# Later copies, joined stores and a longer-spread finish in the scan stage of an attention and selective-scan kernel

## The chip, the cores and the metric

The kernel runs on one core of one Trainium2 chip. The metric is the device time of one execution in microseconds (us). Before the change it is 35322.73 us, the median of three runs (35309.54 to 35332.95).

## The reference

The input x is a 256 x 256 grid of tokens with 128 channels. Layer 0 is a group norm, then row-wise attention with a bias, a mask and a gate, added to x. Layer 1, where the change is, does this on the result (shapes of this case, K = 4 directions, 256 inner channels, 16 states):

```python
xz = x @ w_in.T;  xi, z = split(xz);  z = silu(z)
xc = silu(depthwise_conv3x3(xi) + conv_b)
xs = [rows, columns, rows reversed, columns reversed] of xc      # L = 65536 tokens each
dts, Bs, Cs = split(xs @ x_proj)                                   # 8, 16, 16
delta = softplus(dts @ dt_w + dt_b)
for t in range(L):                                                 # for each direction, channel, state
    h = exp(delta[t] * A) * h + delta[t] * x[t] * B[t]
    y[t] = sum over states of h * C[t]      (+ D * x[t])
y = sum of the four directions, each put back in token order
out = x + (layernorm(y) * z) @ w_out.T
```

## The kernel before, in words

Lines are those of the kernel before. Layer 0 and the projection and convolution take the first fifth of the time and are not touched. What follows is one long software pipeline, written out by hand: within it the order of the instructions on every engine is the order in which the Python program issues them.

**Tiling.** The four directions are done one after the other, in the order 2, 1, 3, 0. A direction has 128 chunks of 512 tokens. A chunk has 8 steps (`g`, 0 to 7); a step does 32 channels x 16 states, laid out as 128 partitions (4 blocks of states x 32 channels) by 4 states (`NI`). So there are 4 scans of 128 x 512 in a step, and 4 *places* (`n`, 0 to 3) in the loop over them, 32 places in a chunk. Place 0 does the fourth state, which is kept apart (`dAl`, `bl`); places 1 to 3 do the others.

**One place** issues on ACT the exponential dA (L983; three PSUM buffers, two SBUF buffers for dAl), then pieces of the side work, then on DVE the scan (L1009). After place 1, DVE multiplies B with delta*x for the next step (`times_B`, L734, from `ur`, which PE spreads at L723). The fourth state gets its B*delta*x by another way: ACT scales a transposed delta*x (`bt`, L693), PE turns it back (`bl`, L705). At the end of a step GpSimd takes up the last state (`hst`, L1025) and multiplies with C in place (L1026, 7 buffers `bx`).

**Sums and copies.** After four steps, half a chunk, PE gathers over states and blocks into a PSUM tile `yp` (`sums`, L749, issued at step 5 for the first half and at step 1 of the next chunk for the second). ACT copies it to SBUF as `yo` (`evacuate`, L922), after which `begin_sums` may use the one `yp` buffer again. This copy is issued at place 0 of step 6 (first half) and of step 2 of the next chunk (second half).

**Side work** is written as generators. Each `yield` ends a piece. `prepare` (started at step 6, two chunks ahead) makes xs, B, C, delta and du = delta*x: copies of the turned x (L595), `pb` and `bc` (L599, L605), softplus by Abs, Relu, Exp and Ln, with Ln at L653, and four GpSimd operations, the last two being delta and delta*x (L659, L662). One piece of it goes to each place, so its Ln is at place 0 of step 2 of the next chunk and delta and delta*x are at place 3 of step 3. Ln and Exp each have a table load on ACT. `turn` (L675, L681) transposes du at step 4, place 3. Each generator in the list `later` gets one piece at every place, before `prepare` does.

**What goes into `later`.** In directions 2, 1 and 3 it is `store`, once per half: PE transposes yo, adding the sum of the directions before (`yl`, loaded by `load_sum`), ACT copies it into half of `yt`, and after the second half it goes to memory. In direction 0 it is `finish`, once per chunk: the sum of all directions (`ysum`, L771 and L776), a copy `ys` (L831), statistics on DVE (L838, L840), their root on GpSimd (`yrs`, `ynb`, L36, L37, L842, L843), normalisation on ACT (`yn`, L847), transposes (`tpz`, L861), weights and bias on ACT (`gz`, L868), the product with z on GpSimd (L872), the output projection with the residual (`po`, L878, L881), and a copy `xo` (L891) to the output.

**Queues.** All loads and stores of this stage go through the SP queue in issue order. PE, ACT, DVE and GpSimd each take their instructions in order too, so an instruction that waits holds what is issued after it on its engine.

Of the kernel before, what the change touches and what calls it, by code (L numbers as in the profile page):

```python
# [16 lines left out]
P = 128  # L17
# [6 lines left out]
DI = 256  # L24
# [42 lines left out]
def attention_and_scan_kernel(  # L67
# [498 lines left out]
        v = ap.rearrange("(i p w) d -> p w i d", p=P, w=S)  # L566
        return [v[:, w, :, :] for w in range(w0, w0 + T // S)]

    loaded, prepared, scanned, summed, turned, products_of = {}, {}, {}, {}, {}, {}

    def load(q):
        k, a = steps[q]
        xt = io.tile([P, 4, DI], F32, name="xtok")
        src = tokens(xc_d, k, a)
        n = 4 // len(src)
        for w, s in enumerate(src):
            nc.sync.dma_start(xt[:, n * w : n * w + n, :], s)
        loaded[q] = xt

    def prepare(q):  # L580

        k, a = steps[q]
        xt = loaded.pop(q)
        xs = io.tile([P, 2, T], F32, name="xs")
        tps = []
        for h in range(2):
            tp = sps.tile([P, T], F32, name="tps", tag="mm")
            for j in range(4):
                nc.tensor.transpose(
                    tp[:, j * P : (j + 1) * P], xt[:, j, h * P : (h + 1) * P], ident  # L590
                )
            tps.append(tp)
            yield
        for h, tp in enumerate(tps):
            nc.scalar.copy(xs[:, h, ::-1] if k >= 2 else xs[:, h, :], tp)  # L595
            yield
        pb = sps.tile([R + 2 * NS, T], F32, name="pb", tag="mm")
        for h in range(2):
            nc.tensor.matmul(  # L599
                pb, xw_in[:, k, h, :], xs[:, h, :], start=(h == 0), stop=(h == 1)  # L600
            )
        yield
        yield
        bc = io.tile([R + 2 * NS, T], F32, name="bc", bufs=1)
        nc.scalar.copy(bc, pb)  # L605
        bc_d = sd.tile([2 * NS, T], F32, name="bc_d")
        nc.sync.dma_start(bc_d, bc[R:, :])
        yield


        e = io.tile([P, 2, T], F32, name="e", bufs=1)
        delta = io.tile([P, 2, T], F32, name="delta", bufs=1)
        pvs = []
        for h in range(2):
            pv = sps.tile([P, T], F32, name="pv", tag="mm")
            nc.tensor.matmul(  # L616
                pv, dtw_s[:, k, h * P : (h + 1) * P], bc[:R, :], start=True, stop=True
            )
            pvs.append(pv)
        yield  # L620
        yield
        for h, pv in enumerate(pvs):
            nc.scalar.activation(e[:, h, :], pv, AF.Abs, bias=dtb_s[:, k, h : h + 1])
            nc.scalar.activation(delta[:, h, :], pv, AF.Relu, bias=dtb_s[:, k, h : h + 1])
            yield
        tp = sps.tile([P, 4, R + 2 * NS], F32, name="tpb", tag="mm")
        for b in range(4):
            nc.tensor.transpose(
                tp[:, b, :], bc[:, b * P : (b + 1) * P], ident[: R + 2 * NS, : R + 2 * NS]
            )  # L630
        nc.scalar.activation(e, e, AF.Exp, scale=-1.0)
        B_r = io.tile([P, NB, T], F32, name="B_r")
        C_r = io.tile([P, NI, T], F32, name="C_r")
        for m, t, ni in ((0, B_r, NB), (1, C_r, NI)):
            for j in range(4):
                n = m * NS + NI * j
                nc.sync.dma_start(
                    t[32 * j : 32 * j + 32],
                    bc_d[n : n + ni, :].unsqueeze(0).to_broadcast([32, ni, T]),
                )  # L640
        yield
        lg = io.tile([P, 2, T], F32, name="lg", bufs=1)
        nc.scalar.activation(lg, e, AF.Identity, bias=1.0)
        yield
        du = io.tile([P, 2, T], F32, name="du")
        nc.scalar.activation(du, lg, AF.Identity, bias=neg_one)
        B_t = io.tile([P, 4, R + 2 * NS], F32, name="B_t")
        nc.scalar.copy(B_t, tp)
        yield
        nc.gpsimd.tensor_tensor(e, e, du, ALU.subtract)  # L650
        yield
        yield
        nc.scalar.activation(lg, lg, AF.Ln)  # L653
        for _ in range(NI - 1):
            yield
        nc.gpsimd.tensor_tensor(lg, lg, e, ALU.add)  # L656
        for _ in range(NI):
            yield
        nc.gpsimd.tensor_tensor(delta, delta, lg, ALU.add)  # L659
        de_d = sd.tile([DI, T], F32, name="de_d")  # L660
        nc.sync.dma_start(de_d.rearrange("(h p) t -> p h t", p=P), delta)
        nc.gpsimd.tensor_tensor(du, delta, xs, ALU.mult)  # L662
        prepared[q] = xs, de_d, du, B_r, C_r, B_t
# [111 lines left out]
            else:  # L775
                nc.tensor.matmul(o, yo, ident, start=False, stop=True, skip_group_check=True)  # L776

    def store(q, yo, h):

        k, a = steps[q]  # L780
        yt, yl = scanned[q], summed.get(q)
        hs_ = slice(h * P, (h + 1) * P)
        yield
        tp = sps.tile([P, 4, P], F32, name="tpy", tag="mm")
        add_sum(
            tp,
            None if yl is None else yl[:, :, hs_],
            [(tp[:, j, :], yo[:, j * P : (j + 1) * P]) for j in range(4)],
        )
        yield  # L790
        yield
        nc.scalar.copy(yt[:, :, hs_], tp)
        if h == 1:
            dst = tokens(y_d[k], k, a)
            n = 4 // len(dst)
            for w, s in enumerate(dst):
                nc.sync.dma_start(s, yt[:, n * w : n * w + n, :])
            del scanned[q]
            summed.pop(q, None)

    def finish(q, yos):

# [1 line left out]

        a = steps[q][1]
        yl = summed.pop(q)

        def rest(n):
            for _ in range(n):
                yield  # L810

        yield
        zt = io.tile([P, 2, T], F32, name="zl", bufs=1)
        nc.sync.dma_start(zt, z_d[:, a : a + T].rearrange("(h p) t -> p h t", p=P))
        sums_ = []
        for g in range(2):
            ps = sps.tile([P, 2, DI], F32, name="ysum", tag="mm")
# [7 lines left out]
                ],  # L825
            )
            sums_.append(ps)
            yield from rest(2)
        ys = io.tile([P, 4, DI], F32, name="ys", tag="yt")
        for g, ps in enumerate(sums_):  # L830
            nc.scalar.copy(ys[:, 2 * g : 2 * g + 2, :], ps)  # L831
            yield
        st = io.tile([P, 4, 6], F32, name="yst")
        mv = io.tile([P, 4, 2], F32, name="ymv")
        rs = io.tile([P, 4], F32, name="yrs")
# [5 lines left out]
        rsqrt(nc, rs, mv[:, :, 1], 1e-5, neg_half)  # L841
        nc.gpsimd.tensor_tensor(nb, mv[:, :, 0], rs, ALU.mult)  # L842
        nc.gpsimd.tensor_scalar(nb, nb, -1.0, None, ALU.mult)  # L843
        yield from rest(3)
        yn = io.tile([P, 4, DI], F32, name="yn", tag="yl")
        for j in range(4):
            nc.scalar.activation(  # L847
                yn[:, j, :],
                ys[:, j, :],
                AF.Identity,  # L850
                bias=nb[:, j : j + 1],
                scale=rs[:, j : j + 1],
            )
            if j % 2:
                yield
        yield
        tps = []
        for h in range(2):
            tp = sps.tile([P, T], F32, name="tpz", tag="mm")
# [2 lines left out]
                    tp[:, j * P : (j + 1) * P], yn[:, j, h * P : (h + 1) * P], ident  # L862
                )
            tps.append(tp)
        yield from rest(2)
        gz = io.tile([P, 2, T], F32, name="gz", bufs=1)
        for h, tp in enumerate(tps):
            nc.scalar.activation(  # L868
                gz[:, h, :], tp, AF.Identity, bias=lnb_s[:, h : h + 1], scale=lnw_s[:, h : h + 1]
            )  # L870
            yield
        nc.gpsimd.tensor_tensor(gz, gz, zt, ALU.mult)  # L872
        yield from rest(11)
        xr = io.tile([P, 4, D], F32, name="xr", bufs=1)
        nc.sync.dma_start(xr, x2_d[a : a + T, :].rearrange("(j p) c -> p j c", p=P))
        yield from rest(12)
        po = sps.tile([P, 4, D], F32, name="po", tag="mm")
        nc.tensor.matmul(po, ident, xr, start=True, stop=True)  # L878
        for j in range(4):
            for h in range(2):  # L880
# [5 lines left out]
                    stop=True,  # L886
                    skip_group_check=True,
                )
        yield from rest(3)
        xo = io.tile([P, 4, D], F32, name="xo", bufs=1)  # L890
        nc.scalar.copy(xo, po)  # L891
        nc.sync.dma_start(out[a : a + T, :].rearrange("(j p) c -> p j c", p=P), xo)
# [27 lines left out]
    def evacuate(q, h):  # L920
        yo = wk.tile([P, T], F32, name="yo", bufs=2)
        nc.scalar.copy(yo[:, ::-1] if steps[q][0] >= 2 else yo, yps.pop((q, h)))  # L922
        yos[q, h] = yo
        if steps[q][0] == ORDER[-1]:
            if h == 1:
                later.append(finish(q, [yos.pop((q, 0)), yos.pop((q, 1))]))
                del prepared[q]
        else:
            if h == 0:
                scanned[q] = io.tile([P, 4, DI], F32, name="yt")  # L930
            later.append(store(q, yos.pop((q, h)), h))
            if h == 1:
                del prepared[q]

    def begin_sums(q, h):
        yps[q, h] = sps.tile([P, T], F32, name="yp", bufs=1)
# [6 lines left out]

    ctx.enter_context(tc.manual_schedule())
    load(0)
    load(1)
    preparing.append(prepare(0))
    drain(preparing)
    preparing.append(turn(0))
    drain(preparing)  # L950
    preparing.append(products(0, 0))
# [12 lines left out]
    for s, (q, g) in enumerate(all_steps):  # L964
        k, a = steps[q]
        nxt = all_steps[s + 1] if s + 1 < len(all_steps) else None
        if g == 1:
            drs[q, 1] = spread_delta(q, 1)
        if k != ORDER[0] and g == (4 if a else 5):
            summed[q] = load_sum(q)  # L970
        if g == 2 and q + 2 < NQ:
            load(q + 2)
# [5 lines left out]
        for n, i in enumerate((NB, *range(NB))):  # L978
# [4 lines left out]
            nc.scalar.activation(  # L983
                dA, dr, AF.Exp, scale=A_s[:, k, g // 4, g % 4, i : i + 1]
            )
            if n == 0 and g == 2 and q:
                evacuate(q - 1, 1)
                begin_sums(q, 0)
            if n == 0 and g == 6:
                evacuate(q, 0)  # L990
                begin_sums(q, 1)
            if n == 0 and g == 1 and q:
# [98 lines left out]
```

## Time and profile before

| stretch of the trace | us | PE | DVE | ACT | GpSimd (POOL) |
|---|---|---|---|---|---|
| whole span | 35280.6 | 74% | 84% | 71% | 73% |
| direction 2 | 6840 | 71% | 95% | 81% | 88% |
| directions 1 and 3 | 13610 | 71% | 96% | 81% | 88% |
| direction 0 | 7650 | 71% | 88% | 77% | 84% |

A chunk takes about 53.5 us in direction 2, 53.3 in directions 1 and 3, and 60.3 in direction 0. The costliest groups are GpSimd's product with C (4542 ns each, 18602.6 us in all), DVE's scans (1266 and 1259 ns, 20221.9 us together), and DVE's product with B (1729 ns, 7080.4 us).

In the lines of a profile, a group or timeline entry gives engine, line of the kernel, operation and tiles; `x4` is a count; a bracket such as `[2.50 <-ACT dA L983]` is the time the engine stood idle just before the instruction and what ended the wait. A line of the waits is "engine, tile, line <- who released it: us in total, times, longest".

### The profile page before, as it was taken

The numbers are of one execution on the slowest core, as the hardware profiler recorded it, in microseconds if no ns is written. First come the engines' busy times: TensorE is split into PE (matmuls) and PEld (weight loads), VectorE is DVE, ScalarE is ACT, GpSimd is POOL, SyncE is SP. The second block draws the span as 40 slices with busy tenths as digits, with TensorE's granted clock in tenths as the row PEclk, the third lists the DMA queues.
The fourth block names the chain that finished last, engine by engine and source line by source line (L and its number), as shares of the span: only waits on it lengthen the run. The fifth ranks groups of instructions, "written<-read, shape, count | busy, mean of one in ns | idle before, by whom it ended". The sixth has DMA issues, their size and how long they took to land.

```text
span 35280.6 us, 352910 instructions
## 1 busy us (share of the span) xinstructions
PE 26226.3 (74%) x109078; PEld 12390.7 (35%) x109078; DVE 29738.4 (84%) x29211; ACT 25019.2 (71%) x50182; POOL 25808.4 (73%) x11291
## 2 busy tenths in 40 slices
PE   5999899967677777777777777777777777777776
PEld 2555544433333333333333333333333333333333
DVE  7666611199999999999999999999999888888888
ACT  3555411188888788888888888888888777777777
POOL 4222200088888888888888888888888888888888
PEclk8999999977777777777777777777777777777777
DMA  3000111144444444444444444444444444444444
GB/s 128 29 29 29 32 62 62 65 104 104 106 104 105 103 105 107 115 114 116 114 115 115 117 115 115 116 114 116 115 116 115 112 109 112 110 109 111 110 111 102
DMA packets 2099611, 3516.78 MB, mean 100 GB/s; under 512 B 201384, under 2 KB 1187368, under 8 KB 2022832
## 3 DMA queue, kind: packets, MB, share of 16 engines
q1 hardware_dynamic: 2094832, 3492.87, 39.3%
q8 instruction: 857, 14.04, 0.2%
q14 instruction: 1042, 8.54, 0.1%
q10 hardware_dynamic: 2880, 1.34, 0.0%
HBM read 2754.17 MB, written 739.25 MB: 99 GB/s over the span
## 4 chain that ended last, share of the span: by engine, by line
POOL 49%; PE 23%; issue 11%; ACT 8%; DVE 8%; POOLq 0%; DMA 0%; ACTq 0%; DVEq 0%; SPq 0%
POOL bx L1026 34%; PE pc L471 6%; POOL du L662 3%; POOL delta L659 3%; PE yp L749 3%; DVE bx L1009 3%; POOL lg L656 2%; PE ur L723 2%; ACT dA L983 2%; DVE bx L734 2%; PE av L341 2%; POOL at L318 2%; POOL hst L1025 1%; ACT bt L693 1%; PE atp L330 1%
## 5 line engine op out<-in xcount | busy, mean ns | idle before, releaser
L1026 POOL TENSOR_TENSOR bx<-bx,C_r 128x2048 f32<-128x2048 f32 x4096 | 18602.6, 4542 | 334.0 <-POOL hst L1025 6.8
L1009 DVE TENSOR_TENSOR_SCAN bx<-dA,hst,bx 128x512 f32<-128x512 f32 x12192 | 15105.8, 1266 | 1234.0 <-ACT dA L983 1234.0
L723 PE MATMUL ur<-du,spread 128*128 128x512 f32 x8192 | 6490.3, 886 | 4357.5 <-DVE bx L734 4357.5
L983 ACT ACTIVATE dA<-dr,A_s 128x512 f32<-128x512 f32 x12288 | 8364.9, 686 | 1484.8 <-DVE bx L1009 1450.7
L734 DVE TENSOR_TENSOR bx<-B_r,ur 128x1536 f32<-128x1536 f32 x4096 | 7080.4, 1729 | 35.7 <-PE ur L723 35.7
L693 ACT ACTIVATE bt<-duT,B_t 128x128 f32<-128x128 f32 x16384 | 5664.6, 399 | 0.0
L1009 DVE TENSOR_TENSOR_SCAN bx<-dAl,hst,bl 128x512 f32<-128x512 f32 x4064 | 5116.1, 1259 | 576.5 <-ACT dAl L983 262.5
L749 PE MATMUL yp<-bx,gather 128*32 128x512 f32 x32768 | 4605.6, 690 | 12.3 <-POOL bx L1026 12.2
L705 PE MATMUL bl<-ident,bt 128*128 128x128 f32 x16384 | 3349.7, 340 | 1233.1 <-DVE bx L1009 1232.8
L705 PEld LDWEIGHTS bl<-ident,bt 128*128 128x128 f32 x16384 | 2317.8, 172 | 3379.3 <-DVE bx L1009 2623.5
L723 PEld LDWEIGHTS ur<-du,spread 128*128 128x128 f32 x8192 | 1695.1, 257 | 4988.9 <-DVE bx L734 4988.8
L1025 POOL COPY hst<-bx 128x4 f32<-128x4 f32 x4096 | 770.0, 188 | 3029.8 <-DVE bx L1009 2872.5
L983 ACT ACTIVATE dAl<-dr,A_s 128x512 f32<-128x512 f32 x4096 | 2936.7, 717 | 0.0
L318 POOL TENSOR_TENSOR at<-at,sm 128x2048 f32<-128x2048 f32 x256 | 922.3, 3603 | 2707.7 <-DVE sm L317 2568.4
L749 PEld LDWEIGHTS yp<-bx,gather 128*32 128x32 f32 x32768 | 1379.9, 126 | 3755.6 <-issue 3459.8
L675 PE MATMUL tpd<-ident,du 128*128 128x128 f32 x4096 | 979.3, 417 | 1842.7 <-POOL du L662 1842.7
L471 PE MATMUL pc<-xi,diag 128*128 128x512 f32 x4608 | 2031.5, 592 | 0.0
L488 DVE COPY xct<-pt 128x512 f32<-128x512 f32 x256 | 177.1, 692 | 1837.8 <-PE pt L487 1837.8
L616 PE MATMUL pv<-bc,dtw_s 8*128 8x512 f32 x2048 | 1201.8, 713 | 629.3 <-ACT bc L605 629.3
L681 ACT COPY duT<-tpd 128x512 f32<-128x512 f32 x1024 | 600.4, 586 | 1478.8 <-PE tpd L675 1478.8
L675 PEld LDWEIGHTS tpd<-ident,du 128*128 128x128 f32 x4096 | 775.0, 217 | 2474.0 <-POOL du L662 2474.0
L922 ACT COPY yo<-yp 128x512 f32<-128x512 f32 x1024 | 597.1, 583 | 1470.0 <-PE yp L749 1469.6
(166 smaller groups left out, 35061.1 us busy)
## 6 DMA issues: line engine op xcount, KB each, us to landing
dr<-de_d SPq DMA_DIRECT2D x4096, 256.0 KB
C_r<-bc_d SPq DMA_DIRECT2D x2048, 256.0 KB
B_r<-bc_d SPq DMA_DIRECT2D x2048, 192.0 KB
de_d<-delta SPq DMA_DIRECT2D x512, 512.0 KB
xtok<-xc_d SPq DMA_DIRECT2D x256, 512.0 KB
xtok<-xc_d SPq DMA_DIRECT2D x512, 256.0 KB
yl<-y_d SPq DMA_DIRECT2D x512, 256.0 KB
y_d<-yt SPq DMA_DIRECT2D x512, 256.0 KB
```

The costliest lines, as they stand in the source:

```text
L318: nc.gpsimd.tensor_tensor(at, at, sm.unsqueeze(3).to_broadcast([P, H, 2, S]), ALU.mult,)
L471: nc.tensor.matmul(pc, diag[:, h, t, :], xi[:, h, 2 * q + dy : 2 * q + dy + 2, dx : dx + S], start=(t == 0), stop=(t == 8),)
L616: nc.tensor.matmul(pv, dtw_s[:, k, h * P : (h + 1) * P], bc[:R, :], start=True, stop=True)
L675: nc.tensor.transpose(tp[:, b, h * P : (h + 1) * P], prepared[q][2][:, h, t0 : t0 + P], ident)
L693: nc.scalar.mul(bt[:, b, :, j, :], duT[:, b, h * P : (h + 1) * P].rearrange("t (g c) -> t g c", c=32), B_t[:, b, n : n + 1],)
L705: nc.tensor.transpose(bl[:, b * P : (b + 1) * P], bt[:, b, g % 4].rearrange("t j c -> t (j c)"), ident)
L723: nc.tensor.matmul(ur, spread[:, g % 4].rearrange("p j c -> p (j c)"), prepared[q][2][:, g // 4, :], start=True, stop=True,)
L734: nc.vector.tensor_tensor(bx[:, :NB, :], prepared[q][3], ur.unsqueeze(1).to_broadcast([P, NB, T]), ALU.mult,)
L749: nc.tensor.matmul(yp[32 * g : 32 * g + 32, :], gather, hc[:, i, :], start=(i == 0 and steps[q][0] != ORDER[0]), stop=True, skip_group_che ...
L983: nc.scalar.activation(dA, dr, AF.Exp, scale=A_s[:, k, g // 4, g % 4, i : i + 1])
L1009: nc.vector.tensor_tensor_scan(hs[:, i, :], dA, hs[:, i, :] if i < NB else bls.pop((q, g)), 0.0 if a == 0 else hst[:, g, i : i + 1], ALU.mult,
L1026: nc.gpsimd.tensor_tensor(hs, hs, prepared[q][4], ALU.mult)
```

## The change

It has four parts.

1. `evacuate` and `begin_sums` go one step later: from step 2 to step 3 (second half of the chunk before) and from step 6 to step 7 (first half). The `yo` copy is meant to meet sums that are done, and no longer to stand just ahead of the Ln at step 2. In consequence xs has three buffers, as `begin_sums` reads it later, and the token tile xtok one; the load of `yl` at a direction's first chunk goes from step 5 to step 7.
2. `store` is done once for both halves, after the second one: both sums at places 1 and 2, both copies two places later, then the store. `yt` is taken only there.
3. `finish` is spread: 58 places instead of 44, counted from place 0 of step 3. The statistics and their root come at step 4, place 2, after GpSimd's delta and delta*x instead of just ahead of them; the four `yn` at four places; `tpz` at step 1 of the chunk after, `gz` at step 2 behind Ln, the product with z at step 4, `po` at step 0 and `xo` at step 1 of the next chunk but one. The loads of z and of the residual are issued later as well.
4. The first load but one is issued after the first `prepare`.

```diff
-        xt = io.tile([P, 4, DI], F32, name="xtok")
+        xt = io.tile([P, 4, DI], F32, name="xtok", bufs=1)
-        xs = io.tile([P, 2, T], F32, name="xs")
+        xs = io.tile([P, 2, T], F32, name="xs", bufs=3)
...
-    def store(q, yo, h):
+    def store(q, yos):
...
+        yl = summed.pop(q, None)
+        yield
+        tps = []
+        for h, yo in enumerate(yos):
+            hs_ = slice(h * P, (h + 1) * P)
+            tp = sps.tile([P, 4, P], F32, name="tpy", tag="mm")
+            add_sum(
...
+            tps.append(tp)
+            yield
+        yield
+        yt = io.tile([P, 4, DI], F32, name="yt")
+        for h, tp in enumerate(tps):
+            nc.scalar.copy(yt[:, :, h * P : (h + 1) * P], tp)
+            yield
+        dst = tokens(y_d[k], k, a)
...
     def finish(q, yos):
...
-        yield
-        zt = io.tile([P, 2, T], F32, name="zl", bufs=1)
-        nc.sync.dma_start(zt, z_d[:, a : a + T].rearrange("(h p) t -> p h t", p=P))
+        yield
...
-            yield from rest(2)
+            yield
+        yield
         ys = io.tile([P, 4, DI], F32, name="ys", tag="yt")
         for g, ps in enumerate(sums_):
             nc.scalar.copy(ys[:, 2 * g : 2 * g + 2, :], ps)
             yield
+        zt = io.tile([P, 2, T], F32, name="zl", bufs=1)
+        nc.sync.dma_start(zt, z_d[:, a : a + T].rearrange("(h p) t -> p h t", p=P))
...
-        yield from rest(3)
+        yield from until(6, 11)
         yn = io.tile([P, 4, DI], F32, name="yn", tag="yl")
-        for j in range(4):
+        for j, now, then in ((0, 11, 12), (1, 12, 16), (2, 16, 17), (3, 17, 26)):
...
-            if j % 2:
-                yield
-        yield
+            yield from until(now, then)
...
-        yield from rest(2)
+        yield from until(26, 29)
         gz = io.tile([P, 2, T], F32, name="gz", bufs=1)
...
+        yield from until(31, 36)
         nc.gpsimd.tensor_tensor(gz, gz, zt, ALU.mult)
-        yield from rest(11)
+        yield from until(36, 40)
         xr = io.tile([P, 4, D], F32, name="xr", bufs=1)
...
-        yield from rest(12)
+        yield from until(40, 55)
...
-        yield from rest(3)
+        yield from until(55, 57)
...
-        if k != ORDER[0] and g == (4 if a else 5):
+        if k != ORDER[0] and g == (4 if a else 7):
...
-            if n == 0 and g == 2 and q:
+            if n == 0 and g == 3 and q:
                 evacuate(q - 1, 1)
                 begin_sums(q, 0)
-            if n == 0 and g == 6:
+            if n == 0 and g == 7:
                 evacuate(q, 0)
                 begin_sums(q, 1)
```

## The prediction

> **What bounds the kernel now.** I read the busy time by stage first, because three of the four directions end in a copy back to memory and the last in the finish. In the answer for the stretches of direction 2, directions 1 and 3, and direction 0 (columns: stretch, length, then PE, PEld, DVE, ACT, POOL busy, clock, DMA share, GB/s):
>
> ```profile
> 7060.00:13900.00 6840.00, 4827.52 (x19374) 2098.44 (x19374) 6520.32 (x5103) 5507.02 (x10706) 5988.14 (x2554) 0.73 0.43 104
> 13950.00:27560.00 13610.00, 9661.75 (x40914) 4352.18 (x40906) 13035.82 (x10223) 11036.19 (x21473) 11994.77 (x5112) 0.75 0.47 115
> 27610.00:35260.00 7650.00, 5407.26 (x23552) 2618.63 (x23551) 6713.80 (x6085) 5910.36 (x11496) 6452.51 (x3169) 0.78 0.45 110
> ```
>
> DVE is busy 95.3%, 95.8% and 87.8%: it bounds the first 384 chunks nearly, the last 128 not. So the question is what its idle time waits for. From the waits of DVE, the second stretch (first line), then the third:
>
> ```profile
> DVE bx L1009 <- ACT dA L983: 565.4, 255, 3.1
> ```
> ```profile
> DVE bx L1009 <- ACT dA L983: 391.4, 253, 3.0
> DVE bx L1009 <- ACT dAl L983: 262.5, 126, 2.9
> DVE bx L1009 <- ACT duT L681: 184.7, 82, 2.6
> DVE bx L1009 <- PE bl L705: 79.4, 97, 1.6
> ```
>
> Directions 1 and 3 have one wait per chunk, 565.4/255 = 2.22 us. (Direction 2, by the same view, 287.7 us on ACT in 127 chunks, some 0.2 us more on others: I use 2.5 in all.) Direction 0 has several, 918.0/127 = 7.23 us. The timeline of one chunk of direction 1 shows where; ACT and, below, DVE:
>
> ```profile
> 21002.47 0.72 ACT L983 ACTIVATE dAl<-dr,A_s 128x512 f32<-128x512 f32 x1
> 21004.73 0.58 ACT L922 COPY yo<-yp 128x512 f32<-128x512 f32 x1 [1.54 <-PE yp L749]
> 21005.33 1.28 ACT L653 ACT_TABLE_LOAD   x1
> 21006.63 1.06 ACT L653 ACTIVATE lg<-lg 128x1024 f32<-128x1024 f32 x1
> 21007.70 1.28 ACT L983 ACT_TABLE_LOAD   x1
> 21009.00 1.91 ACT L983 ACTIVATE dA<-dr,A_s 128x512 f32<-128x512 f32 x3
> ```
> ```profile
> 21009.72 1.28 DVE L1009 TENSOR_TENSOR_SCAN bx<-dA,hst,bx 128x512 f32<-128x512 f32 x1 [2.50 <-ACT dA L983]
> ```
>
> At step 2, place 0, ACT waits for the gather sums (1.54), copies them (yo), and then does Ln between two table loads (3.67 us to the next dA). The three stand in one queue; DVE eats its stock of dA and stands 2.50 us. In direction 0 the same place costs 2.62 us, and the finish adds others:
>
> ```profile
> 31004.97 1.09 ACT L847 ACTIVATE yn<-ys,ynb,yrs 128x256 f32<-128x256 f32 x2 [2.93 <-POOL ynb L843]
> 31018.72 0.78 ACT L868 ACTIVATE gz<-tpz,lnb_s,lnw_s 128x512 f32<-128x512 f32 x1 [4.78 <-PE tpz L861]
> ```
> ```profile
> 31012.01 1.28 DVE L1009 TENSOR_TENSOR_SCAN bx<-dAl,hst,bl 128x512 f32<-128x512 f32 x1 [1.59 <-PE bl L705]
> 31020.72 1.28 DVE L1009 TENSOR_TENSOR_SCAN bx<-dAl,hst,bl 128x512 f32<-128x512 f32 x1 [2.24 <-ACT dAl L983]
> 31022.74 1.28 DVE L1009 TENSOR_TENSOR_SCAN bx<-dA,hst,bx 128x512 f32<-128x512 f32 x1 [0.74 <-ACT dA L983]
> ```
>
> 1.59 + 2.24 + 0.74 + 2.62 = 7.19, the 7.23 of the mean. Read back: POOL waits 1.99 us for the statistics and does their root (1.95 us) ahead of delta and delta*x; so du is late, so PE's tpd and the bl behind it, so DVE (1.59). PE's sums come next, tpz stands behind them, gz waits 4.78 us for tpz, and dAl is behind gz (2.24, 0.74).
>
> **What the Trainium skill says.** "ScalarE: Activation LUTs", What ACT_TABLE_LOAD costs: about 1283 ns a load, and a drain of about 1.38 us more. The trace agrees on the load (1283 ns in each of 512), shows no such drain (0.02 us between load and Ln), and I use the trace's 3.67. "Trace Analysis", Tensor Engine Instruction: ACT, DVE and GpSimd are strict FIFO, and PE's ends are estimated; the first is what the chains above rest on, and for the second, DVE started 0.10 us after the stated end of bl (31011.91), so these ends can be used. "SBUF — State Buffer", Who interferes with whom: a DVE instruction with two SBUF inputs, or in a two-port mode, and GpSimd block each other. bn_stats moves beside other GpSimd work; its 399 to 428 ns here show no blocking, so I move it at its present cost.
>
> **The change part by part.**
> *Copies one step on.* At step 3 the sums are long done, so of the waits for yp (1.54 and, at step 6, 2.72 us in the chunk shown) nothing should be left; the 0.58 us copy stays. ACT starts Ln earlier by at least 1.54 + 0.58 = 2.12, and from step 6 on by up to 2.72 more, as far as three dA buffers allow. Need: 2.50. So DVE's wait for Ln goes to about 0 in directions 2, 1 and 3. Can ACT fall behind again? bc waits for pb, which PE makes 3.1 us after times_B of step 6 (21038.1 to 21041.1 in that chunk); from bc to the dA after Ln ACT has 15.0 + 4.4 us; together 22.5; DVE needs that dA 2.4 + 3 x 6.36 + 1.2 = 22.6 us after times_B (a step without a wait takes 6.36). It just fits: a wait of some tenths may stay, and by the next paragraph it would replace another one, not add to it.
>
> *But that wait was also GpSimd's time to catch up.* A chunk of direction 2 with a short wait for Ln has another after it:
>
> ```profile
> 12047.75 1.28 DVE L1009 TENSOR_TENSOR_SCAN bx<-dA,hst,bx 128x512 f32<-128x512 f32 x1 [0.78 <-ACT dA L983]
> 12066.12 1.28 DVE L1009 TENSOR_TENSOR_SCAN bx<-dAl,hst,bl 128x512 f32<-128x512 f32 x1 [0.36 <-ACT duT L681]
> ```
>
> GpSimd, never idle from step 0 on there (4.54 us a product, 2.35 each for e, lg, delta, du), ends du late, then tpd and bl follow on PE, and DVE stands. 0.78 + 0.36 = 1.14; where the wait for Ln was 1.39 (at 18027.60), there was none. So with no wait for Ln, DVE stands about 1.15 us at step 5. Gain per chunk: 2.5 - 1.15 = 1.35 in direction 2, 2.22 - 1.15 = 1.07 in 1 and 3: 128 x 1.35 + 256 x 1.07 = 173 + 274 = 447 us.
>
> *Both halves stored together, buffers, later loads.* The same matmuls, copies and bytes at other places; the store leaves at step 4, 32 places ahead of its buffer's second use. Nothing on DVE's path: 0.
>
> *Finish spread over 58 places (direction 0).* Statistics move from step 3 place 3 to step 4 place 2, behind du; so the 1.59 goes. tpz moves to step 1 and gz to step 2, behind Ln; so 2.24 + 0.74 go. DVE's bn work stays (4 x 409 + 4 x 151 ns at the group's means, 1.58 us in the timeline), as do four yn of about 0.5 us net. What comes: yn now waits for ynb at step 5, place 3. GpSimd there does the step-3 product, gz*z (2.36) and the root (1.95), so ynb ends 18.6 us after GpSimd takes up step 2's state: 14.2 to the end of that product (21015.08 to 21029.28 in the chunk above, with no pause), 2.4 and 1.95. ACT then has yn, bt, dAl (1.85), 23.0 us of its present work from the dAl of step 6 to that of step 2 (25.60 in the chunk from 31020.69, less a bc wait of 1.88 and a gz of 0.68), plus three yn and xo (2.0), plus Ln to dA (4.4). From that dA, DVE has 5.4 us to the end of step 2. Sum of the loop: 18.6 + 1.85 + 25.0 + 4.4 + 5.4 = 55.3. From the other side, DVE alone needs 60.3 - 7.23 = 53.0; at a period of 55.3 it stands some 2.5 at Ln and 0.3 at step 6. I take 55.5: 128 x 4.8 = 614 us. New PE work ahead of bl: tpz (1.09) at step 1, where bl had about 0.25 us to spare, costs 0.8 at the start of step 2, but there DVE waits for dA after Ln anyway: 0. po (3.6 us at 31002.05) lies in step 0 in the time in which PE waits for times_B: 0. The z load waits on the SP queue for gz*z to free its one buffer, with dr of the next chunk behind it; that is about 31 us after the end of step 0 (0.4 + 28.1 + 2.4), dr is needed at about 50 (ACT's dAl of step 6 at 36, and 13 to 15 us more): 0, unless these 1.5 MB take over 19 us.
>
> *End.* The previous chunk's tpz, gz*z and po come ahead of the last one's, and two loads are exposed: about 12 us more (estimate from 1.1 + 1.6 + 2.4 + 3.1 us and two transfers).
>
> 35322.7 - 447 - 614 + 12 = 34274; I say 34270 us.
>
> **Rivals.**
> (a) DVE becomes the bound everywhere: no waits. 2.5 x 128 + 2.22 x 256 + 7.23 x 128 = 1814 less: 33510. For it: a long Ln wait appears only with the yo wait ahead of it. Against: the 0.78 chunk, and GpSimd's 51 us of work in direction 0 (8 x 4.54 + 5 x 2.35 + 8 x 0.19 + 1.7). Chance 0.13.
> (b) The finish only changes its wait: ynb to yn, on an ACT with less slack, costs what the old chain cost, and direction 0 gains about 1 us a chunk: 35322.7 - 447 - 128 = 34750. For it: ACT is the tightest loop of my sum. Chance 0.15.
> (c) Slower: the z load holds the SP queue so that dr comes late, or PE's added work at steps 0 to 2 delays bl each chunk beyond Ln. With 5 us a chunk in direction 0 on top of today's 60.3 and 250 us gained elsewhere: 35322.7 + 640 - 250 = 35710. For it: GpSimd, ACT and SP all get later due times; against: no wait for dr in the trace, 4 to 8 us of slack by the sums. Chance 0.08.
> (d) Gains and losses cancel, within 70 us: 0.03.
>
> **How the numbers follow.** The forecast with sizes off by up to a third either way: 0.61. Its waits can be 0.8 to 1.5 us in 384 chunks (+-130) and the loop 54 to 57.5 in direction 0 (-190 to +260). The range takes in most of (b) and part of (a): 33750 to 34850. Faster 0.89, same 0.03, slower 0.08.
>
> **What would show it.** ACT's wait for yp at yo gone (1.9 us a time now); DVE's wait for dA in directions 1 to 3 gone and one of about 1.15 us for bl or duT in its place; in direction 0 no wait at gz, one of 3 to 4 us at yn for ynb, and a wait for dA after Ln still there. It would be wrong if yo still waits, if bc's wait for pb puts ACT more than 1 us behind, or if dr appears among the waits.

## The result, and the profile after

The changed kernel takes 34389.54 us (median of four runs, 34388.68 to 34394.71) against 35326.21 us for the kernel before in the same measurement: a ratio of 0.9737, 95% interval 0.9721 to 0.9752. The forecast was 34270 with a range of 33750 to 34850. The kernel before came out at 35278 to 35327 us in the five measurements of this document, so a difference of less than about 50 us between two versions that were not measured together is not to be relied on.

By direction (a chunk's period is the distance of the `bc` copies of the first and last chunk of a stretch, divided by the chunks between; the forecast in the first two rows is the period before, less the gain forecast; DVE's waits are those of the same stretch):

| direction | chunk before | forecast | chunk after | DVE waits before | after |
|---|---|---|---|---|---|
| 2 | 53.63 | 52.3 | 52.90 | 2.47 | 1.75 |
| 1 and 3 | 53.26 | 52.2 | 52.45 | 2.22 | 1.39 |
| 0 | 60.30 | 55.5 | 55.58 | 7.29 | 2.54 |

In the two profiled executions that is 128 x 0.73 + 256 x 0.81 + 128 x 4.72 = 93 + 207 + 604 = 904 us, less some 6 us at the end (34.6 us from the last scan to the end before, 40.6 after); the spans differ by 894.

The busy time of the three stretches of the changed kernel, in the order and columns used for the kernel before:

```profile
7060.00:13870.00 6810.00, 4557.25 (x19546) 2050.08 (x19546) 6581.24 (x5151) 5556.91 (x10811) 6041.30 (x2576) 0.82 0.44 106
13880.00:27270.00 13390.00, 9626.46 (x40854) 4412.24 (x40846) 13034.41 (x10214) 11059.60 (x21449) 11983.43 (x5108) 0.79 0.48 117
27310.00:34350.00 7040.00, 5198.35 (x23484) 2616.37 (x23484) 6707.04 (x6084) 5910.32 (x11490) 6441.56 (x3166) 0.81 0.50 119
```

DVE is busy 96.6%, 97.3% and 95.3%: the same work in less time. PE's granted clock, the column before the last two, is higher than before (0.82, 0.79 and 0.81 for 0.73, 0.75 and 0.78). That alone is not the gain: the run with the copies alone, below, has the same 0.834 over its whole span as the changed kernel and takes 35038 us, and the one with all three edits has 0.854 and takes 35050. What part of the gain comes by way of shorter PE work was not separated.

What DVE still waits for, first in directions 1 and 3, then in direction 0:

```profile
DVE bx L1007 <- ACT dA L981: 252.2, 256, 2.1
DVE bx L1007 <- ACT duT L681: 96.6, 117, 1.1
DVE bx L1007 <- PE bl L705: 6.6, 25, 0.4
```
```profile
DVE bx L1007 <- ACT dA L981: 274.5, 127, 2.7
DVE bx L1007 <- PE bl L705: 37.8, 92, 1.0
```

The waits of direction 0 for dAl (262.5 us before) and for duT (184.7) are gone; that for dA remains, at Ln. In directions 1 and 3 the wait for dA is halved, and one for duT has come, which was 0.6 us in all before. Step 2 of a chunk on ACT no longer has a wait or a copy between dAl and the table load:

```profile
22010.42 0.73 ACT L981 ACTIVATE dAl<-dr,A_s 128x512 f32<-128x512 f32 x1
22011.16 1.28 ACT L653 ACT_TABLE_LOAD   x1
22012.46 1.06 ACT L653 ACTIVATE lg<-lg 128x1024 f32<-128x1024 f32 x1
22013.53 1.28 ACT L981 ACT_TABLE_LOAD   x1
```

And ACT's own waits in directions 1 and 3, before (first line: yo for the sums) and after:

```profile
ACT yo L922 <- PE yp L749: 977.5, 511, 3.0
```
```profile
ACT duT L681 <- PE tpd L675: 913.0, 255, 4.4
ACT xs L595 <- PE tps L589: 369.7, 255, 2.0
ACT bc L605 <- PE pb L599: 200.7, 139, 1.6
```

The 977.5 us at yo are gone, but 570.4 us have come at xs and bc, where ACT did not wait before (its wait for tpd, 794.9 us before, has grown too). ACT now gets to step 6 early and meets PE, whose transposes of x (tps) stand behind the sums and bl. So the lead that ACT gains for Ln is less than the wait removed.

In direction 0 the wait at gz (598.4 us before) is gone, and ACT waits at yn for ynb, as the prediction had it, 471.4/127 = 3.7 us a chunk (371.9/127 = 2.9 before):

```profile
ACT yn L852 <- POOL ynb L848: 471.4, 127, 3.9
```

### The profile page after: what moved, and what is told of

It is laid out like the page before. It is cut to its first block, busy times and chain, and to the rows that moved or that the text cites. A ratio compares the mean times of both kernels' runs of the same rounds, so it can differ in the third digit from the quotient of the medians.

```text
span 34386.9 us, 352916 instructions
## 1 busy us (share of the span) xinstructions
PE 25692.6 (75%) x109078; PEld 12391.1 (36%) x109078; DVE 29744.0 (86%) x29211; ACT 25060.5 (73%) x50182; POOL 25796.5 (75%) x11291
## 4 chain that ended last, share of the span: by engine, by line
POOL 62%; PE 20%; issue 11%; DVE 4%; ACT 3%; POOLq 0%; DMA 0%; ACTq 0%; SPq 0%; DVEq 0%
POOL bx L1024 44%; PE pc L471 6%; POOL du L662 4%; POOL delta L659 3%; POOL lg L656 3%; POOL e L650 2%; POOL hst L1023 2%; PE av L341 2%; POOL at L318 2%; PE yp L749 1%; PE atp L330 1%; PE ur L723 1%; DVE at L305 1%; ACT bt L693 1%; PE sc L298 1%
## 5 line engine op out<-in xcount | busy, mean ns | idle before, releaser
L723 PE MATMUL ur<-du,spread 128*128 128x512 f32 x8192 | 5941.2, 816 | 3917.0 <-DVE bx L734 3914.8
L749 PE MATMUL yp<-bx,gather 128*32 128x512 f32 x32768 | 4337.4, 648 | 9.6 <-POOL bx L1024 7.9
L705 PE MATMUL bl<-ident,bt 128*128 128x128 f32 x16384 | 3117.0, 321 | 1287.8 <-DVE bx L1007 1287.2
L705 PEld LDWEIGHTS bl<-ident,bt 128*128 128x128 f32 x16384 | 2153.0, 162 | 3034.0 <-DVE bx L1007 2350.4
L723 PEld LDWEIGHTS ur<-du,spread 128*128 128x128 f32 x8192 | 1605.2, 244 | 4373.9 <-DVE bx L734 4373.8
L479 ACT ACTIVATE xcs<-pc,cb_s 128x512 f32<-128x512 f32 x256 | 175.9, 687 | 1898.5 <-PE pc L471 1898.5
L650 POOL TENSOR_TENSOR e<-e,du 128x1024 f32<-128x1024 f32 x512 | 1205.8, 2355 | 317.6 <-DMA C_r<-bc_d 317.6
```

The lines of the kernel that those rows point to most:

```text
L705: nc.tensor.transpose(bl[:, b * P : (b + 1) * P], bt[:, b, g % 4].rearrange("t j c -> t (j c)"), ident)
L723: nc.tensor.matmul(ur, spread[:, g % 4].rearrange("p j c -> p (j c)"), prepared[q][2][:, g // 4, :], start=True, stop=True,)
L749: nc.tensor.matmul(yp[32 * g : 32 * g + 32, :], gather, hc[:, i, :], start=(i == 0 and steps[q][0] != ORDER[0]), stop=True, skip_group_che ...
```

## The experiments

All were timed against the kernel before, and the ratio and its interval are to that kernel. "Chunks" below gives the periods in directions 2; 1 and 3; 0, read as in the table above (the changed kernel: 52.90; 52.45; 55.58), each from one traced execution.

### Which part brought what

**Copies alone**, in the kernel before, together with what the change does to buffers (xtok, xs) and to the order of loads (not shown here):

```diff
-            if n == 0 and g == 2 and q:
+            if n == 0 and g == 3 and q:
                 evacuate(q - 1, 1)
...
-            if n == 0 and g == 6:
+            if n == 0 and g == 7:
                 evacuate(q, 0)
```

> The copies of the sums one step on, alone, in the kernel before (with the buffers they need); stores per half and the short finish stay. My theory: in directions 2, 1 and 3 this alone is the whole gain (chunk 52.4 to 52.9 us, as in the changed kernel), and in direction 0 the finish moves along by four places, so its statistics already fall behind delta*x; some waits at gz stay: 56 to 58 us a chunk. In all 34450 to 34650. Rival, the joined store is what frees ACT in directions 2, 1 and 3: their chunks stay above 53, and the total is above 34750.

35038.37 us (ratio 0.993, 0.9915 to 0.9945); chunks 53.53; 52.90; 59.17. My theory's total is missed by far; the rival's has the total, but its chunks above 53 only in direction 2. The copies alone gain 0.10 us a chunk in direction 2, 0.36 in directions 1 and 3 and 1.13 in direction 0. What the changed kernel has beyond this run is the joined store in the first three directions, worth 0.63 and 0.45 us a chunk on top of the copies, and the spread finish in direction 0, worth 3.59. In direction 0, 3.85 of the 6.26 us that DVE waits are for dAl: the short finish in its new place still holds ACT at yn (415.0 us in 121 chunks) and at xo (283.3 us, for po).

**Copies back**, in the changed kernel:

```diff
-            if n == 0 and g == 3 and q:
+            if n == 0 and g == 2 and q:
...
         yl = summed.pop(q)
-        yield
+        yield from until(-4, 1)
```

(Step 7 goes back to 6 likewise, and the first `yield` of `store` is lengthened in the same way, so that store and finish keep their places.)

> The changed kernel with only the copies put back to steps 2 and 6; stores and finish keep their places. My theory: the wait for yp ahead of Ln is back, directions 1 and 3 at 53.2 us a chunk, direction 2 at 53.5, direction 0 loses some 2 us a chunk to it: 34950 in all, within 100. Rival, the copies count for little and the spread finish for most: under 34600.

34649.25 us (0.9818, 0.9801 to 0.9834); chunks 53.26; 52.91; 56.32. That is neither near 34950, as in my theory, nor under 34600. Without the later copies, the rest of the change still gains 0.38, 0.35 and 3.98 us a chunk. The two runs together: in directions 1 and 3, of the gain of 0.81, the copies bring 0.36 alone and 0.46 as the last part, the joined store 0.35 and 0.45. Both runs have the changed buffers and order of loads, which were not tried by themselves. How the store helps can be read from the order, and was not tested further: the yt copy of the first half (0.58 us) stood at step 6 in the stretch in which ACT has no pause before Ln, and now stands at step 4. With the copies back DVE waits 470.6/254 = 1.85 us at dA against 2.22 before. So the prediction's 0 for the joined store was wrong.

### What still holds directions 2, 1 and 3

**GpSimd relieved**: the line `nc.gpsimd.tensor_tensor(e, e, du, ALU.subtract)` left out.

> The changed kernel without GpSimd's e - du (2.35 us a chunk of GpSimd's time ahead of du; the rounding correction of softplus is left out). My theory, GpSimd's work between step 0 and du sets the wait that is left in directions 2, 1 and 3: the waits of 1.4 and 1.75 us there fall to 0.3 or less, direction 0 changes by under 0.5 us a chunk: 33850 to 33950. Rival, ACT with its Ln and tables is what is left: less than 100 us gained.

34228.3 us (0.9699, 0.9684 to 0.9713); chunks 52.56; 51.99; 55.56. The result lies between the two forecasts: 0.34 us a chunk gained in direction 2 and 0.46 in directions 1 and 3. The waits fall to 1.47 and 0.87 us and not to 0.3, and nearly all that is left is at dA (219.3 of 221.3 us in directions 1 and 3). Direction 0 does not move, so there it is not GpSimd's total of work that binds.

**Ln relieved**: `AF.Ln` replaced by `AF.Identity`.

> The changed kernel with a plain copy in place of Ln, so without the two table loads of each chunk (the logarithm of softplus is left out). My theory: ACT has 2.6 us more in each chunk, but in directions 2, 1 and 3 GpSimd keeps DVE waiting 1.0 to 1.4 us, now for bl or duT and no longer for dA, so little is gained (0 to 0.5 us a chunk); in direction 0, where ACT's loop is the longest, about 2 us a chunk. In all 34000 to 34150. Rival, Ln is what DVE waits for in all directions: all dA waits go, about 690 us, 33700.

34217.11 us (0.9696, 0.9681 to 0.971); chunks 52.71; 52.34; 54.61. DVE's waits in directions 1 and 3:

```profile
DVE bx L1007 <- ACT duT L681: 330.2, 253, 2.3
DVE bx L1007 <- PE bl L705: 3.1, 4, 1.3
```

Not one wait for dA is left, and yet DVE waits 1.3 us a chunk, now for duT: in these directions GpSimd's path by du takes over almost in full, as my theory had it. In direction 0 it gains 0.97, half of what I expected, which is why the total is above its range.

**Both left out**:

> The changed kernel without e - du and with a copy for Ln, both left out of softplus at once. Each alone gained 140 to 170 us. Theory, ACT by Ln and GpSimd by du are two bounds of nearly the same length in directions 2, 1 and 3, each covering the other: both out gain far more than the sum, waits under 0.3 us a chunk there, 33700 to 33850. Rival, the gains just add up: 34020 to 34080.

33850.24 us (0.9588, 0.9574 to 0.9602); chunks 51.77; 51.58; 54.22. Against the changed kernel the single runs gain about 161 and 172 us, and both together 539 (the chunk periods give 164, 177 and 541). In directions 1 and 3 it is 0.46 and 0.11 us a chunk singly and 0.87 together, in direction 2 0.34 and 0.19 singly and 1.13 together. DVE's waits in directions 1 and 3 are down to this:

```profile
DVE bx L1006 <- ACT duT L680: 136.2, 253, 1.3
DVE bx L1006 <- PE bl L704: 7.6, 30, 0.6
```

So there are two bounds of nearly one length, Ln on ACT and du from GpSimd. Each alone hides what the other is worth. The waits that I had put at under 0.3 us are still 0.56 in directions 1 and 3 and 0.67 in direction 2.

### Attempts to shorten the paths

**Later yn** in direction 0:

```diff
-        yield from until(6, 11)
+        yield from until(6, 16)
...
-        for j, now, then in ((0, 11, 12), (1, 12, 16), (2, 16, 17), (3, 17, 26)):
+        for j, now, then in ((0, 16, 17), (1, 17, 20), (2, 20, 21), (3, 21, 26)):
```

> The changed kernel with the four yn of the finish five places later (from step 7, place 0). Only direction 0 can change. My theory, ACT's loop over the wait for ynb is what bounds direction 0: the wait of 3.7 us at yn goes, ACT reaches Ln that much earlier, and DVE's 2.5 us a chunk fall to about 1: 34150 to 34300. Rival, GpSimd's 52 us of work hold direction 0 near 55.3 us a chunk: 34330 or more.

34441.75 us (0.9764, 0.9749 to 0.9778); direction 0 at 55.97, so 0.4 us worse. The wait at yn is gone, and ACT waits elsewhere:

```profile
ACT dA L981 <- DVE bx L1007: 417.2, 445, 3.7
ACT duT L681 <- PE tpd L675: 378.4, 126, 3.3
ACT bc L605 <- PE pb L599: 282.4, 125, 3.0
```

For dA buffers it is 417.2 us (177.1 in the changed kernel) and for pb 282.4 (21.5). The time given back at yn was not kept as a lead, and the four yn now lie after bc, in the stretch without pauses ahead of Ln; DVE's wait for dA grows from 2.2 to 2.6. This does not settle whether the loop of the prediction, through ynb and yn, bounds the changed kernel: the edit cuts the loop, but puts four yn into another path that is then as long. GpSimd's 52 us, the rival, are not the bound: 2.35 us less of its work in a chunk left direction 0 at 55.56.

**tpd behind bl** (`turn` begun at step 5, place 0, ahead of the sums, and no longer at step 4, place 3):

> The changed kernel with the transposes of du issued on PE behind the bl of step 5 and not ahead of it. Theory: the wait of DVE for duT at step 5 (0.38 us a chunk in directions 1 and 3, 0.11 in direction 2) goes, but as GpSimd's next product, the sums and the bl of step 6 follow, half of it comes back there or at Ln: 34280 to 34380. Rival, du to bl is the only path from GpSimd: as much as 0.4 us in 384 chunks more at Ln as well, 34200 or less.

34631.8 us (0.9818, 0.9803 to 0.9832); chunks 53.94; 52.93; 55.55: worse. DVE's waits for duT are gone, but ACT's own wait for tpd rises from 913.0 to 1430.6 us in directions 1 and 3, and DVE pays for that with 1.81 us a chunk for dA, where it was 0.99, in two waits: in the chunk at 22007, 1.50 us behind Ln and 0.75 us three steps later. The result lies outside both forecasts.

**Last step's sums last**:

```diff
-        for i in range(NI):
-            for g, hc in enumerate(his):
+        early = [(i, g) for i in range(NI) for g in range(3)]
+        for i, g in early + [(i, 3) for i in range(NI)]:
```

> The changed kernel with the gather sums in another order: the twelve matmuls of the first three steps of a half first, the four of the last step after them, so that less is left for PE when GpSimd's last product lands (3.6 to 4.7 us of sums, of which about 2.4 would be left). Theory, product to sums to bl and tps is one of the two paths that keep DVE waiting in directions 2, 1 and 3, by bl and by way of tps, xs, pb, bc to Ln: 0.5 to 1 us less a chunk there, 34000 to 34200. Rival, PE loses more by the four in one column group than it gains: 34350 to 34600.

35022.09 us (0.9929, 0.9914 to 0.9944); chunks 54.61; 54.05; 55.67. That is worse than the rival had it too: in directions 1 and 3 the sums take 5.4 to 7.0 us, and in the changed kernel 3.6 to 5.8. Two of them in direction 1, each from the timeline of PE and with the view of the same stretch (the third number from the end is the granted clock), the changed kernel first, then the new order:

```profile
14243.45 3.64 PE L749 MATMUL yp<-bx,gather 128*32 128x512 f32 x32
14243.45:14247.09 3.64, 3.64 (x34) 1.01 (x34) 3.64 (x5) 3.64 (x9) 2.23 (x2) 1.00 0.84 200
```
```profile
14263.94 5.38 PE L749 MATMUL yp<-bx,gather 128*32 128x512 f32 x32
14263.94:14269.32 5.38, 5.38 (x34) 1.50 (x34) 5.38 (x6) 5.38 (x14) 3.98 (x2) 1.00 0.84 193
```

The clock is full in both, so the longer time comes with the order. DVE then waits 364.1 us for bl in directions 1 and 3, where it was 6.6.

**All three edits**:

> The three edits of the runs sent with it together: later yn, tpd behind bl, the last step's matmuls last. Theory, the gains add up where they concern different directions and paths: 33800 to 34000. Rival, one bound is behind all three: no better than the best of the three by more than 50.

35049.59 us (0.9936, 0.992 to 0.9953); chunks 54.61; 54.61; 54.62. They do not add up; the total is no better than with the worst of the three alone. Only direction 0 is better than in the changed kernel, by 0.96. That three stretches with different work have one period is taken up in the last section.

**delta*x early**: in `prepare` the four pauses between the sum of lg and e and delta are taken out, so GpSimd does lg, delta and du in one go, ahead of step 2's product.

```diff
         nc.gpsimd.tensor_tensor(lg, lg, e, ALU.add)
-        for _ in range(NI):
-            yield
         nc.gpsimd.tensor_tensor(delta, delta, lg, ALU.add)
```

> The changed kernel with GpSimd's delta and delta*x issued right behind the sum of lg and e (step 2, place 3), so ahead of the products of step 2 and 3 and not behind the former. Theory, the path from GpSimd by du, tpd, bl and duT is one of those that bound directions 2, 1 and 3: du lands 4.8 us earlier, ACT's wait of 3.3 us for tpd and DVE's for duT go; what is left is the path by the step-3 product, the sums and bl or tps, worth about 0.8 us a chunk of waits. 34050 to 34200. Rival, only GpSimd's total up to the step-3 product counts, and it is unchanged: 34340 or more.

34651.32 us (0.9814, 0.9798 to 0.9831); chunks 53.31; 53.71; 54.68. The total is in the rival's range, but not for the rival's reason. ACT's wait for tpd is gone, and direction 0 gains 0.9 us, but direction 2 loses 0.41 and directions 1 and 3 lose 1.26. The groups of PE from 14000 to 27000 us show what happens to the sums, in the changed kernel (first) and here:

```profile
L749 PE MATMUL yp<-bx,gather 128*32 128x512 f32 x15872 | 2205.0, 674 | 1.3
```
```profile
L747 PE MATMUL yp<-bx,gather 128*32 128x512 f32 x15488 | 2583.6, 750 | 426.7 <-POOL bx L1022 426.7
```

PE, no longer held up by tpd, arrives at the sums before GpSimd's last product, stands in the midst of them (426.7 us), and the matmuls are slower, 750 ns for 674. The clock accounts for that: a matmul of the sums that lies wholly in a stretch of full granted clock takes 594 ns in the mean in both kernels, one at half clock 1061 ns, and 26% of them lie at half clock here, 12% in the changed kernel. In one chunk the 26 matmuls after such a wait took 3.62 us (from 22013.72 on, mean clock 1.00), in the next 5.29 (from 22066.27 on, 0.68), and bl and DVE behind them (2.35 us) waited.

**Preparation three places earlier as well**, on top of the edit before:

```diff
-            if g == 6 and n == 0 and q + 2 < NQ:
+            if g == 5 and n == 1 and q + 2 < NQ:
                 preparing.append(prepare(q + 2))
...
-            if n == 0 and g == 5:
-                sums(q, 0)
...
             piece(preparing)
+            if n == 3 and g == 5:
+                sums(q, 0)
```

> The same, and the preparation of a chunk starts three places earlier (step 5, place 1), with the gather sums of the first half issued behind its two transposes of x: ACT's waits for tps and pb should go, and GpSimd's first operation falls into its idle time at step 0, so that the step-3 product lands 1.5 us earlier. Theory, then no path but DVE's own bounds directions 2, 1 and 3: waits under 0.5 us a chunk, 33750 to 33950 in all. Rival, Ln three places earlier meets an ACT with less lead, and its wait grows as the others shrink: 34100 or more.

34076.18 us (0.9652, 0.9638 to 0.9666); chunks 51.54; 51.53; 56.28. In the first three directions this is what the theory asked for: DVE waits 0.33 and 0.44 us a chunk. ACT's wait for tps is gone. Its wait for pb is not: from 14000 to 27000 us it is 582.2 us, where the changed kernel has 200.7 in about the same stretch, and DVE does not feel it. Direction 0 is slower by 0.70 than in the changed kernel, which the theory did not have, and so the total is above its range.

**Mixed**, the earlier preparation in directions 2, 1 and 3 and the order of "delta*x early" in direction 0:

> The early preparation of the run e10_prepare_early for directions 2, 1 and 3, and in direction 0 the order of the run e9_du_early (preparation from step 6, sums at step 5, place 0). Theory, the directions do not depend on each other: 51.5 us a chunk in the first three, 54.7 in direction 0, so 34076 less 128 x 1.6 = 205: 33870, within 50. Rival, chunks of direction 0 owe their 54.7 to something carried over from before, and stay near 56.3: 34080.

33882.13 us (0.9589, 0.9573 to 0.9605), as forecast; chunks 51.55; 51.55; 54.69. Busy time of its three stretches:

```profile
7060.00:13700.00 6640.00, 4855.88 (x19552) 1985.32 (x19551) 6579.19 (x5153) 5568.92 (x10818) 6040.72 (x2577) 0.80 0.45 109
13720.00:26860.00 13140.00, 9943.44 (x40792) 4235.69 (x40791) 13023.00 (x10197) 11020.50 (x21412) 11960.15 (x5099) 0.78 0.49 119
26910.00:33840.00 6930.00, 5127.63 (x23484) 2355.09 (x23484) 6663.27 (x6085) 5903.45 (x11491) 6439.21 (x3167) 0.83 0.51 121
```

DVE is at 99.1%, 99.1% and 96.1%. This version leaves nothing out and beats both kernels; it is 1.5% below the changed kernel's median (33882.13/34389.54 = 0.985, from two measurements).

## Why the prediction was right, and where it was off

**The bound and its waits.** Right. DVE's work in a chunk did not change, and the whole gain is idle time of DVE. By direction, the forecast's 447 us for the first three were 300, its 614 for direction 0 were 604.

**Copies one step on.** Right in kind: the wait for yp at yo is gone, and nothing stands ahead of Ln. But "DVE's wait for Ln goes to about 0" failed: 1.3 us of it stay in direction 2 and 1.0 in directions 1 and 3. The check that ended in "It just fits", with 22.5 us against 22.6, counted pb from times_B only. It took tps for granted, which PE gives late as soon as ACT is early: the new waits at xs and bc (369.7 and 200.7 us) are the likely cause, though no run took away these alone. The forecast also gave the copies the whole gain, 1.35 and 1.07 us a chunk; alone they bring 0.10 and 0.36.

**GpSimd's turn to be late.** Right, and it mattered: without this step the forecast would have been 384 x 1.15 = 442 us lower. With Ln out of the way, DVE waits 1.3 us a chunk for duT, against the 1.15 read from one chunk of the kernel before. It was wrong to treat that as the whole remainder. In the changed kernel every chunk still has a wait at dA and nearly half of them one for duT as well (in the chunk at 22062 it is 0.37 at Ln and 0.82 for duT), and all waits add to 1.39 and 1.75, not 1.15. This is the term that was mis-sized: 0.24 x 256 + 0.6 x 128 = 138 us.

**Stores at no cost.** Wrong, shown by the two runs with the copies alone and the copies back: the joined store is worth 0.35 to 0.45 us a chunk in directions 1 and 3. The forecast's sum was hardly hurt, as it credited the copies with the store's gain too: two errors in part cancel, which is luck.

**The finish.** The three waits named (1.59, 2.24, 0.74) are gone, and 55.58 us a chunk was measured for 55.5. The wait at yn came at 3.7 us, and the one at Ln at 2.2 for the 2.5 expected. But the loop by which I got there, through ynb and yn, was not shown to bind. Taking the wait at yn away gained nothing, in a run that lengthened another path. Taking Ln out, which the loop has in it, gave 54.61; issuing delta and delta*x ahead of the loop gave 54.68, and left 380.4/123 = 3.1 us of the wait at yn. What binds direction 0 stays open, and a right number here is partly luck.

**Hidden work.** tpz ahead of bl at step 1, po at step 0, and the z load with dr behind it: no wait for dr is among those of DVE or ACT, and direction 0's waits for bl are 0.3 us a chunk. Right.

**Rivals.** (a) no waits at all: the mixed run comes near it in the first three directions, but the change itself does not. (b) gave direction 0 a gain of about 1 us a chunk and (c) a loss; it gained 4.72, so neither.

**Open.** Why direction 0 is slower with the early preparation (56.28 for 54.68) was not settled: ACT waits at yn 513.9 us in 122 chunks there, and 380.4 in 123 in the run with delta*x early alone, but taking that wait away in the run with later yn did not help. What the changed buffers and order of loads are worth, and what the clock of PE adds to each of these differences (last section), is open too.

## What to carry to other kernels

When a bubble has two causes of nearly one length, removing either one gains little, and the trace only names the one that came last: take both out in one run to see what they are worth together. A wait taken off an engine that has slack is not yet lead: look where that engine will wait next (here 977.5 us at yo became 570.4 at tps and pb). A single chunk in which the first wait happens to be short is a cheap forecast of what comes in its place (1.15 us read here, 1.3 measured with Ln out).

## What was not expected of the hardware

The same PE instructions take two different times, by the clock granted to PE. In the changed kernel the ur pair took 1.02 us at 22025.63 and 2.08 us at 22018.53, behind 3.36 us of idle time, and at 22056.70, behind 1.71 us. The views of these stretches have the granted clock at full and at half:

```profile
22018.53:22020.61 2.08, 2.08 (x3) 1.04 (x4) 2.08 (x2) 2.02 (x5) 2.08 (x1) 0.50 0.04 8
22025.63:22026.65 1.02, 1.02 (x4) 0.19 (x2) 1.02 (x2) 0.93 (x2) 1.02 (x2) 1.00 0.00 0
22056.70:22058.78 2.08, 2.08 (x6) 0.58 (x10) 2.08 (x2) 2.08 (x5) 0.83 (x1) 0.50 0.39 63
```

The Trainium skill, "TensorE: Matmul & The Clock Gate", Part 1, has this factor of two: the clock is halved after an idle window of about 3.4 us, and the window runs freely. The factor agrees, but the condition is not all of it. At 22050.32 the clock went to half, and in the 3.41 us before PE was busy for 2.60 us and never idle for longer than 0.76. The window shows in the trace: each stretch of one clock lasts a whole multiple of 3.413 us (10.24, 6.83, 3.41 and 17.07 us from 22012.77 on). So a schedule in which PE works in other gaps can have slower matmuls where it waits for nothing longer; in the run with delta*x early this is where the 750 ns for 674 come from, whether or not the stops brought the clock down.

The windows also reach into the period of a chunk, which the experiments were not made for. With all three edits 98% of the chunks last 54.61 us to within 0.1, which is 16 windows, in all three stretches, although DVE waits 2.9, 3.4 and 2.1 us a chunk in them. In direction 2 of the changed kernel two chunks together take 105.81 us, 31 windows, in 95% of cases, and so they do in directions 1 and 3 with the copies alone (94%); before the change three chunks of direction 0 take 180.91, 53 windows (95%). So the period can lock to the clock's windows, and a few tenths of a us a chunk between two runs, the split between copies and store among them, may come from that and not from the edit itself. It does not hold everywhere (in directions 1 and 3 of the changed kernel no two chunks together took 31 windows), and no run changed the clock, so what it costs was not shown.

The gather's order counts as well, at one clock: with the same 16 matmuls, four column groups in turn took 3.64 us at best, and three in turn followed by four matmuls in one group 5.38.
